# Four layers of graph network and experts on one core: the borders between stages are re-ordered

## The chip, the cores and the metric

The kernel runs on one core of a Trainium2 chip. The metric is the device time of one execution in microseconds (us). A core has five engines, each with its own queue that is worked off in order: TensorE (PE; its weight loads are shown apart as PEld), VectorE (DVE), ScalarE (ACT), GpSimd (POOL) and SyncE (SP, which here only issues transfers). [...]

## The reference, cut to what matters

625 nodes with 512 features each go through four layers. Each layer is a graph network on the normalised nodes, and then a feed-forward part of eight experts:

```
x = x + L0_gnn(layernorm(x)); x = x + L0_ffn(layernorm(x))   # mean of neighbours, batch norm; attention, 8 small experts
x = x + L1_gnn(layernorm(x)); x = x + L1_ffn(layernorm(x))   # 2 attention layers, 4 batch norms, layer norm; top-2 of 8 experts
x = x + L2_gnn(layernorm(x)); x = x + L2_ffn(layernorm(x))   # weighted bases, layer norm, relu; 8 small experts, weights from top 2
x = x + L3_gnn(layernorm(x)); x = x + L3_ffn(layernorm(x))   # graph convolution, batch norm, gelu; top-2 of 8 large experts
# batch norm: over the nodes;  layer norm: over the 512 features of a node
# small experts: out = sum over e of comb[:, e] * (gelu(x @ W1[e] + b1[e]) @ W2[e] + b2[e])
```

All arithmetic that counts for time is in float32.

## The kernel before, in words

**Two layouts.** Node-major data lies with 125 nodes on the partitions, in five tiles (`NT = 5`, `T = 125`) of 512 features. Feature-major data lies with 128 features on the partitions, in four blocks (`KD = 4`) of 626 columns, which products take in two halves of 313 (`HC`). `to_features` turns node-major data with 20 transposes on TensorE, four to a tile, and copies each tile out of PSUM with `evac`, which takes VectorE and ScalarE in turn. `to_nodes` turns the other way, with three PSUM tiles of two banks for the five tiles.

**Layer norm** (`LayerNorm`): `add(t, src)` takes the statistics of a tile on VectorE (`bn_stats` L282, `bn_aggr` L283); when the last tile of a group has come, `close` runs a chain of small instructions (`rstd`, L249 to L260: a square root on ScalarE, then four on VectorE) and writes the normalised tiles, in turn on VectorE (L301) and ScalarE (L307). `GROUPS` is tiles 0 to 2 and then 3 and 4; without it all five close together.

**Batch norm** (`BatchNorm`): `add(k)` takes the statistics of a feature block (L410 to L412). At the end of a group of blocks `apply` runs the same chain and then L428 to L430 (or L423 to L426 for one block), after which the blocks are scaled, on ScalarE (L437) and for some on VectorE (L435). `THREE` groups the blocks as 0 to 2 and 3, `TWO` as 0, 1 and 2, 3. `mm_groups` runs the following products in the same groups, so that they can begin on the first.

**Small experts** (`small_experts`, layers 0 and 2): `ahead(e)` is the first product of an expert (eight matmuls, L380) with its gelu on ScalarE (L828); `expert_out` makes, for each of the five tiles, one matmul (L543) and one addition to `x` on VectorE (L545). Two experts run ahead. The last expert's five tiles feed one layer norm over all tiles.

**Router logits** (`node_logits`): eight matmuls for each half of the columns (L455), two copies (L459), five transposes back (L462), then small work on VectorE: a softmax, the choice of two, or the dispatch.

**The graph network of layer 2** (from L1350): for each tile, products with the adjacency (L1353), five matmuls with another matrix (`mm_nodes`, L388 and L391), four partial products, one on VectorE and one on GpSimd (L1362) and two on ScalarE in 16 instructions (L1367), three additions on VectorE (L1371 to L1373) and one on GpSimd (L1369), the statistics, and, later, `finish(t)`: L1342, L1344, L1346 and the statistics of the next norm.

**Order of the queues.** The program is traced in the order of the code. A scheduler then sets each engine's order when the kernel is built: by its own cost model it takes, whenever an engine is free, the first traced instruction that it believes ready. On the chip that order is fixed, and each engine waits for the head of its queue. PSUM holds four tiles (`pstile`) of two banks each. Weights come as 1 MB chunks through SP's queue, three buffers in turn (`take`).

Of the kernel before, what the change touches and what calls it, by code (L numbers as in the profile page):

```python
# [152 lines left out]
def kernel(  # L153
# [111 lines left out]
    class LayerNorm:  # L265
# [14 lines left out]
        def add(self, t, src):  # L280
            self.src[t] = src
            nc.vector.bn_stats(self.st[:, t, :], src)  # L282
            nc.vector.bn_aggr(self.mv[:, t, :], self.st[:, t, :])  # L283
            for lo, hi in self.groups:
                if t == hi - 1:
                    self.close(lo, hi)
# [37 lines left out]
    def to_features(src, name, scale=None, bias=None):  # L324
# [3 lines left out]
        if bias is None:  # L328
            for t in range(NT):
                ps = pstile("ps_tr")  # L330
                for k in range(KD):
# [3 lines left out]
                     ps[:, 0, :KD * T].rearrange("p (k t) -> p k t", t=T), scale)  # L335
        else:
# [60 lines left out]
    class BatchNorm:  # L397
# [3 lines left out]
        def __init__(self, h, groups, gamma, beta, func):  # L401
# [4 lines left out]
            self.bi = small.tile([P, KD], F32, tag="bn_bi", name="bn_bi")  # L406

# [9 lines left out]
        def apply(self, group):  # L417
# [4 lines left out]
            if len(group) == 1:  # L422
# [3 lines left out]
                nc.vector.tensor_mul(sc, r, gamma)  # L426
            else:
                nc.vector.tensor_mul(sc, r, gamma)  # L428
                nc.vector.tensor_mul(bi, self.mv[:, g, 0], sc)
                nc.vector.tensor_sub(bi, beta, bi)  # L430
# [14 lines left out]
    def node_logits(src, w, bias, name):  # L445


        half = P // 2
        wp = small.tile([P, KD, half], F32, tag="lg_w", name="lg_w", bufs=1)
        nc.gpsimd.memset(wp, 0.0)  # L450
        nc.gpsimd.tensor_copy(wp[:, :, :E], w.rearrange("p (k e) -> p k e", e=E))
        ps = pstile("ps_lg")
        for i in range(2):
            for k in range(KD):
                nc.tensor.matmul(ps[k % 2 * half:(k % 2 + 1) * half, i, :HC], wp[:, k, :],  # L455
                                 src[:, k, i * HC:(i + 1) * HC], start=(k < 2), stop=(k >= 2))
        lT = small.tile([P, NP], F32, tag="lg_T", name="lg_T", bufs=1)
        for i, copy in enumerate((nc.vector.tensor_copy, nc.scalar.copy)):
            copy(lT[:, i * HC:(i + 1) * HC], ps[:, i, :HC])  # L459
        pt = pstile("ps_lt")  # L460
        for t in range(NT):
            nc.tensor.transpose(pt[:T, t // 4, t % 4 * P:(t % 4 + 1) * P], lT[:, t * T:(t + 1) * T],  # L462
                                ident)
        lg = stile(name)
        for i, n in ((0, 4), (1, 1)):
            nc.vector.tensor_reduce(
                lg[:, 4 * i:4 * i + n, :],
                pt[:T, i, :n * P].rearrange("p (t g e) -> p t e g", t=n, g=2)[:, :, :E, :],
                axis=AX.X, op=OP.add)
        if bias is not None:  # L470
            nc.vector.tensor_tensor(lg, lg, bias[:, None, :].to_broadcast([T, NT, E]), op=OP.add)
        return lg
# [65 lines left out]
    def expert_out(blocks, comb, e, ln=None):  # L538

        for t in range(NT):  # L540
            ps = pstile("ps_eo")
            for f, (h, w) in enumerate(blocks):
                nc.tensor.matmul(ps[:T, 0, :], h[:, t * T:(t + 1) * T], w, start=(f == 0),  # L543
                                 stop=(f == len(blocks) - 1))
            nc.vector.scalar_tensor_tensor(x[:, t, :], ps[:T, 0, :], comb[:, t, e:e + 1],  # L545
                                           x[:, t, :], op0=OP.mult, op1=OP.add)
            if ln is not None:
                ln.add(t, x[:, t, :])

# [5 lines left out]
    def rows_out(xn):  # L555

        for part, hbm in by_node(rows_hbm):
            nc.scalar.dma_start(hbm, xn[part])
        return to_features(xn, "xnT")
# [257 lines left out]
    def small_experts(src, comb, b1, layer, hpool, ln):  # L817

        hs, ws = {}, {}

        def ahead(e):
            g, j = divmod(e, 4)
            if j == 0:
                ws[g] = take(2)
            w1 = ws[g][0]
            ps = mm_features([(w1[:, k, j * P:(j + 1) * P], src[:, k, :]) for k in range(KD)])
            hs[e] = hpool.tile([P, NP], F32, tag="h", name="h")
            nc.scalar.activation(halves(hs[e]), ps, AF.Gelu_apprx_tanh, bias=b1[:, e:e + 1])  # L828

        bias = expert_bias(comb, layer)  # L830
        bias.pop(0)()
        for e in range(2):
            ahead(e)
        for e in range(E):
            if e + 2 < E:
                ahead(e + 2)
            for step in bias[3 * e - 3:3 * e] if e else ():
                step()
            expert_out([(hs.pop(e), ws[e // 4][1][:, e % 4, :])], comb, e,
                       ln if e == E - 1 else None)  # L840
# [259 lines left out]
    for o in range(KD):  # L1100
        ps = mm_features([(wl[:, k, o * P:(o + 1) * P], agg[:, k, :]) for k in range(KD)])
        nc.vector.tensor_add(halves(hT[:, o, :]), halves(hT[:, o, :]), ps)
        bn.add(o)
# [48 lines left out]
    gate = softmax8(node_logits(yT, vec("L0_ffn_gate_W"), row("L0_ffn_gate_b"), "lg"))  # L1152
    with tc.tile_pool(name="l1g", bufs=1) as pool:
# [11 lines left out]
        with tc.tile_pool(name="l0h", bufs=4) as hpool:  # L1165
            small_experts(yT, gate, vec("L0_ffn_b1"), 0, hpool, LayerNorm(xn))
# [42 lines left out]
        xT = to_features(xn, "xT")  # L1209
        for l in range(2):  # L1210
            if l == 1:
                normalise()
            with tc.tile_pool(name=f"l1p{l}", bufs=2) as pt_pool, \
                    tc.tile_pool(name=f"l1s{l}", bufs=4) as s_pool:
                (w,) = take(1)
                qT = ttile("qT")
                for o, ps in enumerate(mm_groups(
                        TWO, KD, lambda o, k: w[:, k, o * P:(o + 1) * P], xT)):
# [242 lines left out]
```

## Time and profile before

| | |
|---|---|
| median of 3 runs | 1681.29 us (1680.88 to 1683.44) |
| the profiled execution: its own time, and its span from first to last instruction | 1681.51 us, 1679.7 us |
| PE, DVE, ACT, POOL busy | 1505.1, 673.9, 375.8, 256.1 us |
| mean granted TensorE clock | 0.947 |

The profiled execution took 0.2 us more than the median and 1.8 us more than its own span. The stages that the change touches lie, in us from the start of the span, at about 116 to 151 (layer 0's batch and layer norm), 279 to 384 (its small experts, the norm, the queries of layer 1), 511 to 551 and 694 to 760 (the ends of layer 1's two attention layers), 1015 to 1160 (layer 2) and 1177 to 1223 (layer 3's graph network and logits). The two long stages of routed experts, about 774 to 985 and from 1239 on, and the attention are not touched.

A line of the timeline has: start, duration, engine, line, operation, output<-inputs, shapes, count; in brackets how long the engine was idle before it and what ended that. A line of the table by stretches has the stretch, its length, and the busy time and number of instructions of PE, PEld, DVE, ACT and POOL, then the granted TensorE clock, the share of the DMA engines and GB/s.

### The profile page before, as it was taken

What the parts mean: (1) busy time and instruction counts of PE and PEld (TensorE: products, weight loads), DVE (VectorE), ACT (ScalarE), POOL (GpSimd) and SP (SyncE); (2) the same over time, 40 slices, a digit from 0 to 9 for tenths busy, and PEclk for the clock granted to TensorE, in tenths of its full rate; (3) what the DMA queues carried; (4) which work ended last, traced back from release to release, by engine and by line L of the source; (5) the groups of instructions that cost most, each with busy time, mean ns of one, the idle gap of its engine ahead of it and who ended that gap; (6) DMA issues with size and microseconds to landing.
All of it is one profiled execution on the core that took longest, in us unless ns stands there. A gap on an engine that the chain in (4) does not pass through costs nothing.

```text
span 1679.7 us, 15622 instructions
## 1 busy us (share of the span) xinstructions
PE 1505.1 (90%) x5622; PEld 851.1 (51%) x5622; DVE 673.9 (40%) x1754; ACT 375.8 (22%) x704; POOL 256.1 (15%) x309
## 2 busy tenths in 40 slices
PE   7997999989898989846999969698769999999996
PEld 5774556555565656633444436454534444444443
DVE  9825562454884258463222225655421111111110
ACT  1122272111661046321111115311310000000000
POOL 2030042110540034202111112101000001000010
PEclk8998999999999989967999989799879999999998
DMA  3010200111001100063989732014348888869871
GB/s 137 9 47 26 75 1 26 50 51 53 23 1 42 59 26 1 5 260 126 333 260 351 261 71 93 25 51 175 131 155 291 315 301 304 290 265 362 296 260 50
DMA packets 40213, 237.53 MB, mean 141 GB/s; under 512 B 4781, under 2 KB 4909, under 8 KB 14369
## 3 DMA queue, kind: packets, MB, share of 16 engines
q1 hardware_dynamic: 30775, 215.20, 34.9%
q0 software_dynamic: 6608, 15.99, 4.2%
q10 hardware_dynamic: 2746, 5.25, 1.0%
q8 instruction: 48, 0.79, 0.2%
q14 instruction: 36, 0.29, 0.1%
HBM read 246.52 MB, written 14.26 MB: 155 GB/s over the span
## 4 chain that ended last, share of the span: by engine, by line
PE 69%; DVE 13%; issue 11%; DMA 4%; ACT 2%; POOL 1%; SPq 0%; POOLq 0%; DVEq 0%; ACTq 0%
PE ps_mf L380 13%; PE ps_y L762 10%; PE ps_h L1416 10%; PE ps_mn L388 7%; PE ps_h L1284 5%; PE ps_s L865 4%; PE ps_eo L543 4%; PE ps_o L929 4%; DMA sumsL<-slots,node 3%; PE ps_mg L369 3%; PE ps_p L908 3%; PE ps_tr L332 2%; DVE s L871 2%; DVE ln_st L282 2%; PE ps_t L753 1%
## 5 line engine op out<-in xcount | busy, mean ns | idle before, releaser
L1416 PE MATMUL ps_h<-ring,xgT 128*128 128x512 f32 x624 | 275.8, 597 | 0.8 <-DVE xgT L226 0.8
L762 PE MATMUL ps_y<-ring,hT 128*128 128x512 f32 x536 | 239.3, 593 | 0.9 <-issue 0.9
L1416 PEld LDWEIGHTS ps_h<-ring,xgT 128*128 128x128 f32 x624 | 119.0, 192 | 148.7 <-issue 146.5
L762 PEld LDWEIGHTS ps_y<-ring,hT 128*128 128x128 f32 x536 | 97.5, 190 | 103.4 <-issue 102.5
L894 POOL TENSOR_SCALAR s<-s,rs 125x625 f32<-125x625 f32 (+4 forms) x120 | 103.3, 877 | 292.1 <-DVE rs L891 268.0
L770 POOL DMA_INDIRECT sumsL<-slots,node x27 | 42.7, 1581 | 466.7 <-DVE slots L768 356.0
L1419 ACT ACTIVATE g<-ps_h 128x512 f32<-128x512 f32 x39 | 23.3, 597 | 388.9 <-PE ps_h L1416 357.7
L1284 PE MATMUL ps_h<-ring,xgT 128*128 128x512 f32 x224 | 102.2, 604 | 1.5 <-DVE xgT L226 0.8
L876 ACT ACTIVATE s<-s,mn 125x626 f32<-125x626 f32 (+4 forms) x120 | 87.3, 743 | 54.1 <-DVE mn L871 53.9
L871 DVE CUSTOM_DVE_ANT_0 s<-ps_s,mask 125x626 f32<-125x626 f32 (+4 forms) x120 | 82.6, 718 | 25.9 <-PE ps_s L865 24.1
L865 PE MATMUL ps_s<-kT,qT 64*125 64x313 f32 (+4 forms) x416 | 87.3, 468 | 2.8 <-DVE mn L871 2.8
L332 PE MATMUL ps_tr<-ident,xn 125*128 125x125 f32 x140 | 30.5, 401 | 66.1 <-DVE ln_nb L304 52.3
L226 DVE COPY hT<-ps_t 128x512 f32<-128x512 f32 x26 | 18.0, 692 | 171.5 <-PE ps_t L753 171.5
L1421 DVE TENSOR_TENSOR h<-ps_h,g 128x512 f32<-128x512 f32 x39 | 26.7, 686 | 148.9 <-ACT g L1419 148.9
L908 PE MATMUL ps_p<-ident,s 125*125 125x125 f32 x432 | 66.5, 296 | 13.0 <-POOL s L894 11.0
L908 PEld LDWEIGHTS ps_p<-ident,s 125*125 125x125 f32 x432 | 54.7, 197 | 39.0 <-POOL s L894 27.1
L1284 PEld LDWEIGHTS ps_h<-ring,xgT 128*128 128x128 f32 x224 | 43.1, 194 | 55.9 <-issue 52.9
L543 PE MATMUL ps_eo<-w,h 128*125 128x512 f32 x160 | 70.8, 593 | 0.6 <-ACT h L828 0.6
L886 DVE SCALAR_TENSOR_TENSOR s<-s,cnt 125x626 f32<-125x626 f32 x80 | 67.3, 863 | 9.9 <-ACT s L876 9.8
L929 PE MATMUL ps_o<-pT,v 125*64 125x375 f32 (+2 forms) x448 | 60.1, 413 | 9.0 <-DVE mn L871 4.2
L1007 PE MATMUL ps_a<-dst,src 125*128 125x313 f16 x400 | 58.2, 310 | 6.7 <-DVE dst L1004 5.1
L768 DVE TENSOR_SCALAR slots<-ps_y,gate 128x512 f32<-128x512 f32 x27 | 20.3, 751 | 106.3 <-PE ps_y L762 106.3
(353 smaller groups left out, 2048.2 us busy)
## 6 DMA issues: line engine op xcount, KB each, us to landing
ring<-in_weights SPq DMA_DIRECT2D x195, 1024.0 KB
w<-in_weights SPq DMA_DIRECT2D x27, 1024.0 KB
rows_hbm<-xn ACTq DMA_DIRECT2D x2, 1120.0 KB
sumsL<-x ACTq DMA_DIRECT2D x2, 1120.0 KB
out<-sumsL SPq DMA_DIRECT2D x1, 1250.0 KB
x<-in_x SPq DMA_DIRECT2D x1, 1120.0 KB
x<-sumsL SPq DMA_DIRECT2D x5, 224.0 KB
rows<-in_rows SPq DMA_DIRECT2D x1, 1052.0 KB
```

The source lines that it names most:

```text
L380: nc.tensor.matmul(ps[:, half, :HC], w, r[:, half * HC:(half + 1) * HC], start=(n == 0), stop=(n == last))
L388: nc.tensor.matmul(ps[:T, 0, :width], src[:, k, t * T:(t + 1) * T], w[:, k, :width], start=(k == 0), stop=(k == KD - 1 and extra is None))
L543: nc.tensor.matmul(ps[:T, 0, :], h[:, t * T:(t + 1) * T], w, start=(f == 0), stop=(f == len(blocks) - 1))
L762: nc.tensor.matmul(ys[b][:, 0, :], hT[:, j, :], ring[n % RING][:, j, :], start=(c == 0 and j == 0), stop=(c == nch - 1 and j == 3))
L865: nc.tensor.matmul(ps[hh][:T, i, :w], qT[rr, b, t * T:(t + 1) * T], kT[rr, b, i * w:(i + 1) * w], start=True, stop=True)
L871: nc.vector.tensor_tensor_reduce(s[:, hh, :nb * w].rearrange("p (a c) -> p a c", a=nb), ps[hh][:T, :nb, :w], mask[:, t, :nb * w].rearrange ...
L876: nc.scalar.activation(s[:, hh, :nb * w], s[:, hh, :nb * w], AF.Exp, bias=mn[:, hh:hh + 1], scale=-1.0, accum_out=sm[:, hh:hh + 1] if caus ...
L894: nc.gpsimd.tensor_scalar(s[:, hh, :w], s[:, hh, :w], rs[:, hh:hh + 1], 1.0, op0=OP.mult, op1=OP.mult)
L908: nc.tensor.transpose(pp[:T, hh, j * T:(j + 1) * T], s[:, hh, j * T:(j + 1) * T], ident[:T, :T])
L929: nc.tensor.matmul(po[rr, 0, o:n * T], v[:, j, h * DH:(h + 1) * DH], pT[:, hh, j, o:n * T], start=(j == 0), stop=(j == nk - 1))
L1284: nc.tensor.matmul(ps[:, 0, :], xgT[:, k, :], w1[:, k, :], start=(k == 0), stop=(k == KD - 1))
L1416: nc.tensor.matmul(ps[:, i, :], xgT[:, k, :], w[i][:, k, :], start=(k == 0), stop=(k == KD - 1))
```

## The change

- **Batch norm**: `behind()` puts the VectorE instructions of the blocks that follow a closed group behind the last instruction of that group's chain in VectorE's queue. It is used in all six batch norms.
- **Small experts**: three experts run ahead, not two. Experts 0 to 4 add as before. The last three go tile by tile: expert 5's product is scaled on ScalarE and added to `x` on GpSimd, two tiles ahead; experts 6 and 7 are added on VectorE, then the tile's statistics. The norm closes in two groups.
- **First nodes' products**: `to_features` calls `between` after tile 2. There the products of the first half of the columns are traced, ahead of the transposes of tiles 3 and 4: the logits' (layers 1, 2, 3), two experts' (layer 2), three of four query blocks' (layer 1, whose weights are taken earlier).
- **Layer 1's last norm**: tiles 3 and 4 get their statistics on ScalarE (`add_scalar`, five instructions a tile), their scaling on ScalarE, and gamma and the sum on GpSimd; tiles 0 to 2 stay on VectorE. It closes in two groups.
- **Layer 2's graph network**: the adjacency product and the partial products of tile t + 1 are traced ahead of the other product of tile t; one addition moves from VectorE to GpSimd; the norm closes in groups of 2, 2 and 1; `finish` is called for 0, 1, then 2 and 3, then 4.

The diff, cut to its core:

```diff
 class LayerNorm:
+        def add_scalar(self, t, src, junk):
+            self.src[t] = src
+            acc = small.tile([T, 3], F32, tag="ln_acc", name="ln_acc")
+            nc.scalar.activation(junk, src, AF.Identity, accum_out=acc[:, 0:1])
+            nc.scalar.activation(acc[:, 1:2], acc[:, 0:1], AF.Copy, scale=-1.0 / D)
+            nc.scalar.activation(junk, src, AF.Square, bias=acc[:, 1:2], accum_out=acc[:, 2:3])
+            nc.scalar.activation(self.mv[:, t, 0:1], acc[:, 0:1], AF.Copy, scale=1.0 / D)
+            nc.scalar.activation(self.mv[:, t, 1:2], acc[:, 2:3], AF.Copy, scale=1.0 / D)
+            self.closed(t)
...
 def to_features(src, name, scale=None, bias=None, between=None):
+                if between is not None and t == GROUPS[0][1] - 1:
+                    between(dst)
...
 class BatchNorm:
+        def behind(self):
+            return nullcontext() if self.chain is None else tc.issue_after(self.chain.ins)
...
+    class Logits:
...
+        def half(self, src, i):
...
             for k in range(KD):
-                nc.tensor.matmul(ps[k % 2 * half:(k % 2 + 1) * half, i, :HC], wp[:, k, :],
+                nc.tensor.matmul(self.ps[k % 2 * h:(k % 2 + 1) * h, i, :HC], self.wp[:, k, :],
                                  src[:, k, i * HC:(i + 1) * HC], start=(k < 2), stop=(k >= 2))
+            copy = nc.scalar.copy if i else nc.vector.tensor_copy
+            copy(self.lT[:, i * HC:(i + 1) * HC], self.ps[:, i, :HC])
...
-    def rows_out(xn):
+    def rows_logits(xn, w, bias):
...
+        lg = Logits(w, bias)
+        lg.half(to_features(xn, "xnT", between=lambda xnT: lg.half(xnT, 0)), 1)
+        return lg.result()
...
+    class SmallExperts:
...
+        def half(self, e, src, i):
...
+            for k in range(KD):
+                nc.tensor.matmul(self.ps[e][:, i, :HC], self.ws[g][0][:, k, j * P:(j + 1) * P],
+                                 src[:, k, i * HC:(i + 1) * HC], start=(k == 0), stop=(k == KD - 1))
+            if i == 1:
+                self.hs[e] = self.hpool.tile([P, NP], F32, tag="h", name="h")
+                nc.scalar.activation(halves(self.hs[e]), self.ps.pop(e)[:, :, :HC],
+                                     AF.Gelu_apprx_tanh, bias=self.b1[:, e:e + 1])
...
+        def run(self, src, comb, ln):
...
+            for e in range(E - 3):
+                self.ahead(e + 3, src)
+                for step in bias[3 * e - 3:3 * e] if e else ():
+                    step()
+                for t in range(NT):
+                    add(e, t)
+            yw = ktile("yw")
+            for n in range(NT + 2):
+                if n < NT:
+                    nc.scalar.activation(yw[:, n, :], self.out(E - 3, n), AF.Copy,
+                                         scale=comb[:, n, E - 3:E - 2])
+                    nc.gpsimd.tensor_add(x[:, n, :], x[:, n, :], yw[:, n, :])
+                if n >= 2:
+                    t = n - 2
+                    add(E - 2, t)
+                    add(E - 1, t)
+                    ln.add(t, x[:, t, :])
...
             for o in range(KD):
                 ps = mm_features([(w[:, k, o * P:(o + 1) * P], oT[:, k, :]) for k in range(KD)])
-                nc.vector.scalar_tensor_tensor(halves(hT[:, o, :]), ps,
-                                               vec("L1_gnn_bo", l)[:, o:o + 1],
-                                               halves(xT[:, o, :]), op0=OP.add, op1=OP.add)
-                bn.add(o)
+                with bn.behind():
+                    nc.vector.scalar_tensor_tensor(halves(hT[:, o, :]), ps,
+                                                   vec("L1_gnn_bo", l)[:, o:o + 1],
+                                                   halves(xT[:, o, :]), op0=OP.add, op1=OP.add)
+                    bn.add(o)
...
+        (wq,) = take(1)
+        xT = to_features(xn, "xT", between=lambda src: [query(o, src, 0) for o in range(KD - 1)])
...
-        ln, after = LayerNorm(), LayerNorm(xn, groups=GROUPS)
+        ln, after = LayerNorm(groups=GROUPS), LayerNorm(xn, groups=GROUPS)
         turned = list(to_nodes(xT, TWO))
+        gamma = row("L1_gnn_ln_g")
+        for t, ps in turned[3:]:
+            ln.add_scalar(t, ps, y[:, t, :])
+        for t, ps in turned[:3]:
+            ln.add(t, ps)
+        for t, ps in turned[3:]:
+            nb = small.tile([T, 1], F32, tag="ln_n", name="ln_n")
+            nc.scalar.activation(nb, ln.mean(t), AF.Copy, scale=ln.r[:, t:t + 1])
+            nc.scalar.activation(nb, nb, AF.Copy, scale=-1.0)
+            nc.scalar.activation(y[:, t, :], ps, AF.Identity, scale=ln.r[:, t:t + 1], bias=nb)
+            nc.gpsimd.tensor_mul(y[:, t, :], y[:, t, :], gamma)
+            nc.gpsimd.tensor_add(x[:, t, :], x[:, t, :], y[:, t, :])
...
-        ln = LayerNorm(groups=GROUPS)
+        ln = LayerNorm(groups=((0, 2), (2, 4), (4, NT)))
...
             for b in range(2):
                 for h in range(H):
                     nc.scalar.activation(part[b][:, h, :], ag[:, b, :], AF.Copy,
                                          scale=wv[:, h, b:b + 1])
-            nc.gpsimd.tensor_add(part[3], part[3], part[1])
+                nc.gpsimd.tensor_add(part[3], part[3], part[b])
+            parts[t] = part
+        weighted(0)
+        for t in range(NT):
+            if t + 1 < NT:
+                weighted(t + 1)
+            pr = mm_nodes(xnT, wres, t, extra=(ones16[:6, :T], cbs))
+            for done in ((), (), (0,), (1,), (2, 3))[t]:
+                finish(done)
...
             nc.vector.tensor_add(ov, part[2], pr.rearrange("p (h f) -> p h f", h=H))
-            nc.vector.tensor_add(ov, ov, part[0])
             nc.vector.tensor_add(ov, ov, part[3])
             ln.add(t, o[:, t, :])
-            for done in ((), (), (0,), (1, 2), (3, 4))[t]:
-                finish(done)
+        finish(NT - 1)
...
+        def half(src, i):
+            lg.half(src, i)
+            for e in range(2):
+                experts.half(e, src, i)
+        xnT = to_features(xn, "xnT", between=lambda src: half(src, 0))
+        half(xnT, 1)
+        lg = lg.result()
+        experts.ahead(2, xnT)
```

## The prediction

> **What bounds the kernel now.** I read the page first, then the table by stretches, then the timeline of each border. The chain of waits on the page gives TensorE 69% and VectorE 13%:
>
> ```profile
> PE 69%; DVE 13%; issue 11%; DMA 4%; ACT 2%; POOL 1%; SPq 0%; POOLq 0%; DVEq 0%; ACTq 0%
> ```
>
> The table by stretches shows where TensorE stands idle.
>
> ```profile
> 344.50:367.00 22.50, 17.17 (x50) 9.35 (x50) 19.01 (x36) 5.04 (x7) 4.28 (x4) 0.85 0.25 94
> 511.00:548.00 37.00, 27.72 (x98) 18.79 (x96) 18.92 (x62) 6.87 (x12) 0.10 (x1) 0.91 0.16 57
> 531.00:534.00 3.00, 2.91 (x6) 1.93 (x7) 1.00 (x6) 1.83 (x4) 0.00 (x0) 0.50 0.48 202
> 732.00:758.00 26.00, 11.60 (x56) 9.23 (x56) 18.85 (x56) 5.77 (x10) 0.00 (x0) 0.60 0.76 306
> 1056.00:1080.00 24.00, 9.37 (x44) 6.30 (x45) 17.61 (x48) 5.20 (x11) 1.78 (x3) 0.64 0.12 44
> 1138.00:1160.00 22.00, 16.68 (x51) 8.83 (x50) 18.92 (x36) 5.00 (x8) 3.86 (x3) 0.92 0.49 191
> 1239.20:1484.00 244.80, 244.80 (x651) 114.34 (x652) 28.76 (x43) 21.69 (x38) 15.89 (x13) 0.99 0.80 280
> ```
>
> The routed experts (last row) leave TensorE no idle time, so time won before them moves them forward whole. At the borders TensorE idles for length minus busy: 5.3, 9.3, 14.4, 14.6 and 5.3 us in the longer rows, and by the same table 9.4 at 694 to 732 and 11.1 at 1194 to 1222: 69.4 in all, the most that the change can work on.
>
> **Batch norm (layer 1).** The timeline after the first attention:
>
> ```profile
> 526.96 0.17 DVE L260 RECIPROCAL rs_r<-rs_v 128x3 f32<-128x3 f32 x1
> 528.19 0.87 DVE L1241 SCALAR_TENSOR_TENSOR hT<-ps_mf,vecs,xT 128x626 f32<-128x626 f32 x1 [1.06 <-PE ps_mf L380]
> 528.98 0.15 DVE L428 TENSOR_TENSOR bn_sc<-rs_r,vecs 128x3 f32<-128x3 f32 x1
> 529.95 0.14 DVE L430 TENSOR_TENSOR bn_bi<-vecs,bn_bi 128x3 f32<-128x3 f32 x1
> 530.13 2.51 ACT L437 ACTIVATE hT<-hT,bn_bi,bn_sc 128x626 f32<-128x626 f32 x3 [3.81 <-DVE bn_bi L430]
> 531.09 6.08 PE L369 MATMUL ps_mg<-hT,w 128*128 128x313 f32 x16 [2.94 <-ACT hT L437]
> ```
>
> Block 3's L1241 sits in the queue before L428 and waits 1.06 us for TensorE; ScalarE and then TensorE wait for what is behind it. In layer 0's uninterrupted chain ScalarE starts 0.80 us after L260 (132.42 to 133.22). So it starts at 527.76, 2.37 earlier, and its first block (2.51 / 3) is there at 528.6, where TensorE's last product has just ended (528.15). Nothing is late behind it: L1241's product is not there before 528.19. After the idle 2.94 us the granted clock was 0.50 (531 to 534) and 16 records took 6.08 us; the row of the queries, 64 in 16.91, makes 4.23. With a gap of 0.5 the clock should hold. Block 3 follows: statistics by 530.0, ScalarE free at 530.3, scaled at 532.6, two products to 533.8 against 537.2: 3.4 us. If the clock is low all the same, 2.4. Twice: 6.8 (4.8 to 7.0).
>
> [...]
>
> In the second norm (`TWO`) the chain of blocks 0 and 1 is mixed with blocks 2 and 3 and ends 7.75 us after the first L1254 (539.40 to 547.15). Kept whole it ends after 5.3: blocks 0 and 1 take 3.6 (two times 0.87, 0.47, 0.47 and aggregates), the chain 1.7 (131.49 to 133.22). The next queries start 2.4 earlier. What gets late is blocks 2 and 3, done 11.4 us after instead of 10.3; eight products of 0.53 in each half cover that in layer 0 of the two. In the last one only ten transposes do, and to_nodes ends 0.6 later. 2.4 (0.8 to 2.6); the 0.6 is in the last norm below.
>
> Layers 0 and 3: no interruption today (L251 to L430 run through at 131.49 and 1194.87, the next block's product comes after). Nothing; cover is not needed.
>
> **Small experts' ends.** TensorE's last 15 products start at 1137.76, the transposes 18.4 later (344.33 and 362.69 in layer 0: the same):
>
> ```profile
> 1137.76 13.04 PE L543 MATMUL ps_eo<-w,h 128*125 128x512 f32 x30
> 1156.12 3.77 PE L332 MATMUL ps_tr<-ident,xn 125*128 125x125 f32 x20 [5.32 <-DVE xn L301]
> ```
>
> Tile by tile, tile 2's last product is the 11th: 11 x 0.86 = 9.5. Addition 0.73, statistics 0.86, chain 1.19 (1154.33 to 1155.52), L301 0.55: transposes from 12.9, 5.4 earlier, just as the products end. VectorE then still owes four additions (0.66), two statistics (0.7), two copies out of PSUM (0.68), a chain: tile 3 at 18.7, where today its transposes begin at 20.6. So the end lies between 1.9 earlier, if nothing stands between, and 5.4. In layer 0 twelve query products (0.53 each, 6.3 us) are traced there: copies of tile 2 done at 15.6, products to 21.9, tiles 3 and 4 with three of the four PSUM tiles held and so one after the other to 24.1, 20 products to 34.7, against 39.8 (384.12). That is 5.1; I take 4.0 (1.9 to 5.1) for late copies. In layer 2 the scheduler may pull a node product (3.43) in: 3.5 (1.9 to 5.4).
>
> The added wait: expert 6's addition waits for GpSimd's, and behind it queue expert 7's, the statistics, and TensorE by its four PSUM tiles. x is there after 0.86 + 0.77 (L236, 500 columns with pointers) + 1.4 (L1400, 1396 ns) = 3.1 with hops, the product of expert 6 at 3.4; then 1.4 a tile against TensorE's 2.6. Hidden by the products; uncovered it is 2.2 a tile. The queries' weights are taken earlier, so SP also queues the next two loads earlier; the chunk's buffer is free after expert 3, 8.5 us before these 15 products, and 1 MB at 434 GB/s (715 to 718) takes 2.4. Nothing. Three experts ahead: the same products in another order, nothing. Layer 0's logits: copies and transposes of L1160 fill TensorE, nothing.
>
> **Layer 1's last norm.** ScalarE needs for a tile 0.59 and 0.19 (copy, read of an accumulator), 0.63 and 0.19 (L1129), three small ones of 0.21 and waits: 2.3; two tiles 4.6 after to_nodes. Chain 1.2, scaling 1.2 a tile, GpSimd four times 1.4, statistics, chain: tile 4 is normalised 29.7 us after the first L1254, now 29.9. No gain there, but tiles 0 to 2 come before it, are turned and their logits' half (1.45 us) is done. A trap: engines reading different banks of one PSUM tile wait for one another, as in
>
> ```profile
> 284.04 0.68 DVE L226 COPY cnt<-ps_ct 125x500 f32<-125x500 f32 x1
> 284.76 0.27 ACT L234 COPY cnt<-ps_ct 125x125 f32<-125x125 f32 x1 [1.78 <-DVE cnt L226]
> ```
>
> so VectorE's tile 2 waits for ScalarE's tile 3 (one PSUM tile): its first group closes at about 25 and not 21, still before tile 4. Logits' reduction at 34.1 instead of 36.3 (759.58): 2.0 (-1.0, GpSimd slowed, to 3.0). The transfers of rows stay ahead of the copies in ScalarE's queue, as now.
>
> **Layer 2.** TensorE is full to 1055.6 and stays so. VectorE then works through to 1072:
>
> ```profile
> 1065.15 2.76 PE L332 MATMUL ps_tr<-ident,xn 125*128 125x125 f32 x12 [9.52 <-DVE ln_nb L304]
> 1070.04 0.65 DVE L226 COPY xnT<-ps_tr 128x500 f32<-128x500 f32 x1
> 1070.69 0.65 DVE L226 COPY xnT<-ps_tr 128x500 f32<-128x500 f32 x1
> 1072.80 1.92 PE L332 MATMUL ps_tr<-ident,xn 125*128 125x125 f32 x8 [4.90 <-DVE ln_nb L304]
> 1074.66 3.50 PE L455 MATMUL ps_lg<-xnT,lg_w 128*64 128x313 f32 x16
> ```
>
> From 1051.8 it loses two additions (1.3), and the rest of finish 0 and 1 and a part of tile 4 (3.8), which now fit before; it gains L1342 and a third chain (1.5): 3.6, of which I count 2.5 for waits on the last product. Products of two experts' halves (4.2) and the logits' (1.7) then lie before the last eight transposes, and fill up to the 4.9 idle plus 1.5 around the logits; if the copies come as late as at 1070.04, only 1.5. Sum 4.0 to 8.9; 6.0. GpSimd takes 4.0 a tile (1.47 + 2 x 1.27) under TensorE's 6.15. Beside it VectorE is slow:
>
> ```profile
> L1372 DVE TENSOR_TENSOR o<-o,part x5: 669/1708/1748, 1031.9 to 1060.6; 125x512 f32<-125x512 f32 x5
> ```
>
> That add goes; L1373 may inherit it (1.0 each, hidden under TensorE except the last).
>
> [...]
>
> Layer 3's logits: 0.3 (0 to 0.6), the 0.59 idle before 1216.16.
>
> **Sum.** 6.8 + 2.4 + 4.0 + 3.5 + 2.0 + 6.0 + 0.3 = 25.0 (12.4 to 32.6). The profiled execution took 1681.5 (0.2 over the median): 1656.5, ends 1649 and 1669.
>
> **Rivals.** *Early products hide nothing*: copies out of PSUM stand late in VectorE's queue, as at 1070.04. Then 9.2 from batch norm, 1.9 at each end, 2.5 in layer 2: 15.5, 1666. 0.16. *GpSimd on VectorE's path* (slower): 19 added GpSimd instructions (ten at the ends, four in the norm, five in layer 2) of 1.39 and ten ScalarE feeds of 0.77 are 34.1 us; waited out in full, 1690.6. It decides from 73% of that (25.0). For it: 1708 against 669 ns; against: the products' slack above. 0.06. *All borders close*: half of 69.4 us, 1646.8. 0.08. *Nothing happens* because the queues already run so: 1681, against it the 1.06 us wait; 0.02. My forecast has 0.68. About 0.2%, 3.4 us, is what a measurement of this kernel can tell from no change. Faster 0.91, same 0.03, slower 0.06. The range of the sum, widened to the third rival: 1647 to 1669.
>
> **What would show it.** L428 directly after L260 and a clock near 1 in L369; first transposes 13 us after the last 15 products start; experts' products before the last eight transposes in layer 2. Wrong if L545 waits for GpSimd, if L1372's slowness moves to L1373 or L1344 behind 1052, or if TensorE idles as long at these borders.

## The result and the profile after

The changed kernel takes 1683.81 us (median) against 1682.59 us before: ratio 1.0007, interval 1.0001 to 1.0014. The forecast was 1656.5 us, range 1647 to 1669. The change costs 1.2 us where 25.0 were to be won, and the range is missed by 15 us.

The profiled execution after took 1683.31 us, its span 1681.2 us. The chain of waits on its page gives TensorE less than before and "issue" more:

```profile
PE 65%; issue 15%; DVE 12%; DMA 4%; ACT 2%; POOL 1%; ACTq 0%; SPq 0%; POOLq 0%; DVEq 0%
```

The table by stretches of the changed kernel, each stretch as long as the one shown before and moved to the same work (end of layer 0, layer 1's batch norms, last norm, layer 2's norm, end of layer 2):

```profile
346.15:368.65 22.50, 16.37 (x44) 8.20 (x43) 17.81 (x39) 7.52 (x11) 11.45 (x9) 0.86 0.13 47
515.84:552.84 37.00, 32.27 (x109) 21.48 (x108) 21.13 (x65) 8.72 (x13) 0.10 (x1) 0.92 0.16 57
728.90:754.90 26.00, 8.31 (x34) 6.00 (x35) 16.80 (x55) 9.86 (x29) 5.44 (x4) 0.50 0.73 288
1054.70:1078.70 24.00, 11.89 (x40) 7.71 (x40) 16.27 (x48) 3.49 (x8) 0.00 (x0) 0.64 0.12 44
1137.00:1159.00 22.00, 16.80 (x49) 8.40 (x48) 18.03 (x38) 7.87 (x12) 11.67 (x10) 0.89 0.36 146
```

In the second row TensorE's idle time falls from 9.3 to 4.7 us: the batch norms work. At the two ends it does not fall (5.3 to 6.1, 5.3 to 5.2), and in the last norm it grows (14.4 to 17.7: 1.8 us of that lie inside the turn to nodes, 1.4 ahead of the logits). In layer 2 it falls from 14.6 to 12.1, with the clock at 0.64 as before.

Cut at fixed pieces of TensorE's work, read from the timelines, the spans divide as follows. "Again" is a second profile of the same program, and "alone" the kernel before with `behind()` alone; both are told of below.

| stretch, from mark to mark | before | after | again | alone | forecast |
|---|---|---|---|---|---|
| start to layer 0's attention | 207.58 | +1.59 | -0.01 | -0.64 | 0 |
| to layer 0's last expert product | 149.80 | +0.23 | +0.24 | +0.01 | 0 |
| layer 0's end: to the end of the queries | 26.59 | +4.26 | +3.27 | -0.04 | -4.0 |
| layer 1's two attentions | 289.28 | -2.28 | +1.26 | +0.25 | 0 |
| its two first batch norms | 20.00 | -7.04 | -7.05 | -7.04 | -6.8 |
| second batch norm and queries, l = 0 | 28.65 | -0.87 | -2.35 | -3.92 | -2.4 |
| second batch norm and turn to nodes, l = 1 | 14.42 | +1.02 | +1.02 | +1.03 | +0.6 |
| last norm, to the first transposes | 14.30 | +0.11 | +0.11 | -0.44 | -2.6 |
| its logits and choice | 12.42 | +1.99 | +2.42 | -0.08 | (in the row above) |
| dispatch, routed experts | 247.60 | -0.25 | -0.33 | -0.34 | 0 |
| layer 2 to its last expert product | 140.16 | +0.29 | -1.02 | +0.20 | -6.0 |
| layer 2's end: to the end of the node products | 26.10 | +1.43 | +2.34 | +0.04 | -3.5 |
| layer 3 to its first transposes | 35.85 | -0.20 | -0.19 | +0.01 | 0 |
| its logits and choice | 13.63 | +1.66 | +1.95 | +0.01 | -0.3 |
| dispatch, routed experts | 453.31 | -0.42 | +0.18 | -0.48 | 0 |

The rows sum to the difference of the spans: +1.5, +1.8 and -11.4. The three rows of batch norms come to -6.9, -8.4 and -9.9, where -8.6 was forecast. In the column after, every other part lost: 4.3 at layer 0's end, 2.1 in the last norm and logits, 0.3 in layer 2 and 1.4 at its end, 1.7 in layer 3's logits.

**Batch norm after.** The timeline at the place shown before:

```profile
531.80 0.18 DVE L260 RECIPROCAL rs_r<-rs_v 128x3 f32<-128x3 f32 x1
532.60 2.51 ACT L459 ACTIVATE hT<-hT,bn_bi,bn_sc 128x626 f32<-128x626 f32 x3 [1.44 <-DVE bn_bi L452]
533.57 5.03 PE L386 MATMUL ps_mg<-hT,w 128*128 128x313 f32 x16 [0.57 <-ACT hT L459]
```

ScalarE starts 0.80 us after L260, as forecast, and TensorE waits 0.57 instead of 2.94 us.

**The end of layer 0 after.** L315, L321, L347 and L1344 were L301, L307, L332 and L1260:

```profile
358.11 0.30 ACT L249 ACTIVATE rs_s<-ln_mv,eps 125x3 f32<-125x3 f32 x1 [2.05 <-DVE ln_mv L283]
358.82 0.74 DVE L875 SCALAR_TENSOR_TENSOR x<-ps_eo,sm_p,x 125x512 f32<-125x512 f32 x1
...
361.75 0.14 DVE L260 RECIPROCAL ln_r<-rs_v 125x3 f32<-125x3 f32 x1
...
362.55 2.85 PE L347 MATMUL ps_tr<-ident,xn 125*128 125x125 f32 x12 [3.36 <-DVE xn L315]
362.57 4.03 POOL L1344 TENSOR_TENSOR x<-x,rows 125x512 f32<-125x512 f32 x3 [6.46 <-DVE ln_nb L318]
...
364.28 1.12 DVE L257 TENSOR_TENSOR rs_v<-rs_v,rs_r 125x2 f32<-125x2 f32 x1
...
365.43 1.18 DVE L258 TENSOR_TENSOR rs_v<-rs_v,rs_s 125x2 f32<-125x2 f32 x1
...
367.38 0.67 DVE L226 COPY xT<-ps_tr 128x500 f32<-128x500 f32 x1
...
368.16 8.72 PE L1279 MATMUL ps_mg<-xT,w 128*128 128x313 f32 x24 [2.77 <-issue]
...
376.72 0.59 PE L347 MATMUL ps_tr<-ident,xn 125*128 125x125 f32 x4
```

Four things are to be seen. The first chain takes 3.78 us from L249 to the end of L260, not 1.19: additions of tiles 3 and 4 (L875) run in between. In the second chain L257 and L258 take 1.12 and 1.18 us where 0.15 is usual, while GpSimd works on L1344. The copy of tile 2 (L226) out of PSUM, the memory that TensorE writes (the names with `ps_`), stands behind that chain, and TensorE waits for it 2.77 us. Then 24 query records take 8.72 us (6.4 at the rate before), and tile 3, normalised since 367.4, is turned only at 376.7.

**Layer 1's logits after**, TensorE's timeline:

```profile
747.63 2.76 PE L347 MATMUL ps_tr<-ident,xn 125*128 125x125 f32 x12 [14.41 <-DVE ln_nb L318]
751.84 2.35 PE L484 MATMUL ps_lg<-xnT,lg_w 128*64 128x313 f32 x8 [1.45 <-ACT xnT L234]
754.12 1.39 PE L347 MATMUL ps_tr<-ident,xn 125*128 125x125 f32 x8
756.23 1.27 PE L484 MATMUL ps_lg<-xnT,lg_w 128*64 128x313 f32 x8 [0.49 <-ACT xnT L234]
```

TensorE waits 1.45 us for the copy of tile 2, spends 2.35 on half the logits at a granted clock of 0.50, and only then turns tiles 3 and 4, which ScalarE and VectorE had finished by 750.0. Before, it waited for copies once at this border (0.59 us, ahead of the last transposes); now it waits three times, 1.45, 0.49 and, ahead of the last three of those transposes, 0.51 us.

**Layer 2's norm after**, TensorE's timeline where the idle times of 9.52 and 4.90 us were:

```profile
1065.22 2.75 PE L347 MATMUL ps_tr<-ident,xn 125*128 125x125 f32 x12 [10.92 <-DVE ln_nb L318]
1069.42 2.35 PE L484 MATMUL ps_lg<-xnT,lg_w 128*64 128x313 f32 x8 [1.44 <-DVE ln_mv L283]
1071.70 6.43 PE L853 MATMUL ps_h<-xnT,w 128*128 128x313 f32 x16
1077.97 0.59 PE L347 MATMUL ps_tr<-ident,xn 125*128 125x125 f32 x4
```

The first wait is 1.40 us longer. The early products then fill the second, and the last transposes stand behind them.

### The profile page after: what moved, and what is told of

It is laid out like the page before. It is cut to its first block, busy times and chain, and to the rows that moved or that the text cites. A ratio compares the mean times of both kernels' runs of the same rounds, so it can differ in the third digit from the quotient of the medians.

```text
span 1681.2 us, 15705 instructions
## 1 busy us (share of the span) xinstructions
PE 1506.5 (90%) x5622; PEld 848.3 (50%) x5622; DVE 670.2 (40%) x1752; ACT 390.3 (23%) x739; POOL 281.4 (17%) x328
## 4 chain that ended last, share of the span: by engine, by line
PE 65%; issue 15%; DVE 12%; DMA 4%; ACT 2%; POOL 1%; ACTq 0%; SPq 0%; POOLq 0%; DVEq 0%
PE ps_y L783 10%; PE ps_h L1531 10%; PE ps_mf L397 8%; PE ps_h L1378 5%; PE ps_mn L405 5%; PE ps_h L853 4%; PE ps_s L921 4%; PE ps_o L985 4%; DMA sumsL<-slots,node 3%; PE ps_eo L867 3%; PE ps_p L964 3%; PE ps_mg L386 2%; DVE s L927 2%; PE ps_a L1063 1%; PE ps_t L774 1%
## 5 line engine op out<-in xcount | busy, mean ns | idle before, releaser
L226 DVE COPY hT<-ps_t 128x512 f32<-128x512 f32 x26 | 18.0, 692 | 171.5 <-PE ps_t L774 171.5
L347 PE MATMUL ps_tr<-ident,xn 125*128 125x125 f32 x140 | 28.9, 375 | 61.4 <-DVE ln_nb L318 48.5
L748 POOL DMA_INDIRECT slots<-rows_hbm,node x31 | 30.9, 996 | 205.4 <-PE ps_x L760 87.8
```

## The experiments

**One part alone.** The kernel before, with this in five of the six batch norms; layer 3's, for which nothing was forecast, stays as it was:

```diff
+            with bn.behind():
                 nc.vector.scalar_tensor_tensor(...)
                 bn.add(o)
```

> The kernel before, with behind() alone added in all six batch norms and nothing else changed. Theory (the batch norm part works, the other parts give it back): between the two traces layer 1's batch norms moved by -3.4, -0.9, -3.6 and -2.3 us and the turn to nodes after the last gave 1.0 to 3.3 back, so 7 to 10 us less than before, about 1673. Rival (what batch norm wins is waited out again at the next border, whatever the other parts do): within 2 us of before, about 1681.

1671.85 us against 1682.26: ratio 0.9938 (0.9921 to 0.9954). Column "alone" above: outside the batch norms each border is within 0.5 us of before. So this part is worth 10 us, nothing waits it out again, and the other parts together, with `behind()` in layer 3, cost 12.

**Products behind all five tiles.**

```diff
-                if between is not None and t == GROUPS[0][1] - 1:
+                if between is not None and t == NT - 1:
```

> The changed kernel, with the first nodes' products traced behind the transposes of all five tiles again (between is called after the last tile). Theory (early products stand in TensorE's queue before transposes that are ready, and wait themselves for a late copy of tile 2): layer 0's queries end 3.6 us earlier (no wait for the copy at 367.4, no second run of transposes at 376.7), layer 1's logits 2.0 and layer 3's 1.7 earlier, layer 2's experts 1.0 later: about -6 us, 1677 to 1678. Rival (the early products do hide idle time, and GpSimd in VectorE's way is what costs): not faster, or slower by 2 to 5 us, 1684 to 1689.

1679.15 against 1682.26: ratio 0.9978 (0.9968 to 0.9988); 4.7 us under the changed kernel's median. Layer 0's end takes 28.44 us (30.85 and 29.86 with early products), layer 1's logits 11.97 (14.41 and 14.84), below the 12.42 of before. But layer 3's logits take 16.08, longer still, and layer 2 up to its last expert product has 139.43 (140.45 and 139.14): there the early products neither win nor lose. So the theory is right for two borders of four, with 1.4 to 2.4 us at layer 0's end where it said 3.6, and layer 3 goes against it; the whole stays 1 us above the 1677 to 1678 expected. TensorE's timeline there shows why:

```profile
1214.04 2.36 PE L484 MATMUL ps_lg<-xnT,lg_w 128*64 128x313 f32 x8
1216.98 0.79 PE L492 MATMUL ps_lt<-ident,lg_T 128*125 128x128 f32 x2 [0.59 <-DVE lg_T L487]
1217.70 2.35 PE L484 MATMUL ps_lg<-xnT,lg_w 128*64 128x313 f32 x8
```

Two transposes that wait for VectorE's copy of the first half stand ahead of the second half's products.

**Both copies behind both halves**, on top of that run:

```diff
-            copy = nc.scalar.copy if i else nc.vector.tensor_copy
-            copy(self.lT[:, i * HC:(i + 1) * HC], self.ps[:, i, :HC])
         def result(self):
+            for i, copy in enumerate((nc.vector.tensor_copy, nc.scalar.copy)):
+                copy(self.lT[:, i * HC:(i + 1) * HC], self.ps[:, i, :HC])
```

> The run with the products behind all five tiles, with one more edit: the two copies of the logits out of PSUM are traced behind the products of both halves, as before the change. Theory (both halves are banks of one PSUM tile, so the second half's products wait for VectorE's copy of the first, and the scheduler puts transposes between them; 7.5 us from the first product to the reduction in layer 3, 5.1 before): layer 3's logits 2.4 us earlier than without this edit, 1676 to 1678. Rival (the clock of 0.50 is what costs there): within 0.5 us, 1679.

1676.82 against 1681.61: ratio 0.9969 (0.9959 to 0.9979). The sixteen records run without a break, and layer 3's logits take 14.62: 1.5 of the 2.4 us expected. The rest is the length of these records:

```profile
1211.57 4.44 PE L484 MATMUL ps_lg<-xnT,lg_w 128*64 128x313 f32 x16
```

The same records in the same order took 3.46 before, at a granted clock of 0.66, and 3.03 in a later run of this edit, where the stretch is 13.21; sixteen took 2.33 at 1.00 (below), and eight 2.35 at 0.50 in the changed kernel. By these numbers 4.44 stands for a clock little above 0.50, an estimate. So both theory and rival have a share.

**The first layer norm chain kept whole at the two ends:**

```diff
+                    with ln.behind():
                         add(E - 2, t)
                         add(E - 1, t)
                         ln.add(t, x[:, t, :])
```

> The changed kernel, with the first layer norm chain kept whole at the small experts' ends: VectorE's additions and statistics of tiles 3 and 4 are put behind the last small instruction of the chain of tiles 0 to 2. Theory (the chain is cut up by the additions that follow, 3.8 us from its first to its last instruction where an uninterrupted one takes 1.2): the first transposes come 2.6 us earlier in layers 0 and 2, of which 1 to 2.6 each is kept: 1679 to 1682. Rival (what ends last at these ends is the second chain and the copy of tile 2 behind it, held up by GpSimd's additions): first transposes earlier, but queries and node products within 0.5 us of where they were, 1683 to 1684.

1680.34 against 1682.26: ratio 0.9984 (0.9975 to 0.9994). The first transposes start 1.33 us after the last product instead of 3.36:

```profile
358.93 1.96 PE L352 MATMUL ps_tr<-ident,xn 125*128 125x125 f32 x12 [1.33 <-DVE x L880]
```

What they wait for is now an addition of an expert (L880), which reads a PSUM tile, and no longer the normalised tile. Layer 0's end takes 27.25 us, 2.6 to 3.6 less than with the chain cut; layer 2's 27.06, 0.5 to 1.4 less. The cut chain was a cost.

**GpSimd's additions held back.** A small GpSimd copy reads the normalised tile 3, and the additions that follow each end are queued behind it:

```diff
+        held = nc.gpsimd.tensor_copy(small.tile([T, 1], F32, ...), xn[:, 3, 0:1])
...
+                with tc.issue_after(held.ins):
                     nc.gpsimd.tensor_add(x[:, t, :], x[:, t, :], row("L1_gnn_ln_b"))
```

> The changed kernel; at the small experts' two ends GpSimd's additions to x that follow (L1344, L1517) are put behind a small GpSimd copy that reads the normalised tile 3, so that they no longer run beside VectorE's second chain. Theory (GpSimd's additions hold up VectorE's small instructions with two inputs: L257 and L258 took 1.12 and 1.18 us there, 0.16 without GpSimd, and in layer 2 L315 1.25 instead of 0.55): those go back to 0.16 and 0.55, the second chain is 2.0 us shorter in layer 0 and 2.6 in layer 2; queries 1 to 2 earlier, node products 1 to 1.5 earlier: 1680 to 1682. Rival (these instructions are long because of ScalarE or the clock, or nothing waits for them): the same durations, or 1683 to 1684.

1678.41 against 1681.61: ratio 0.9979 (0.997 to 0.9989), lower than the 1680 to 1682 expected. The two ends together are 3.7 us shorter than in either profile of the changed kernel; the rest lies spread over the other stretches. The timeline at the end of layer 0:

```profile
363.24 0.15 DVE L257 TENSOR_TENSOR rs_v<-rs_v,rs_r 125x2 f32<-125x2 f32 x1
363.42 0.16 DVE L258 TENSOR_TENSOR rs_v<-rs_v,rs_s 125x2 f32<-125x2 f32 x1
...
364.57 6.15 POOL L1347 TENSOR_TENSOR x<-x,rows 125x512 f32<-125x512 f32 x5
```

L257 and L258 are back at 0.15 and 0.16; in layer 2, where they had taken 1.04 and 1.20 and L315 1.25, all three are back at 0.16, 0.16 and 0.55. Layer 2's end takes 24.87 us: 2.7 to 3.6 under the changed kernel and 1.2 under before. Layer 0's takes 29.79, near its two values with early products (30.85, 29.86), since its copy of tile 2 is no longer late but tiles 3 and 4 still wait behind 24 query records. So L257, L258 and L315 were longer with GpSimd's additions beside them than without; how the additions do it, no run shows. Not every VectorE instruction beside L1344 was longer: in the changed kernel L253 (362.93) took 0.16 us and the copy L226 (363.68) 0.68.

**All four edits together:** the four diffs above in one kernel.

> The changed kernel with four edits together: products behind all five tiles, both logits copies behind both halves, GpSimd's additions held back at the two tails, and the first layer norm chain kept whole there. Theory (what the two ends lost is the sum of the cut chain, the additions beside the second chain and the early queries): from the last expert product to the end of the queries layer 0 takes 26.6 us less 0.5 to 2 (before 26.6, changed 30.9), and layer 2 to the end of the node products 24 to 25 us (before 26.1, changed 27.5); with the gains of the products behind all tiles that makes 1670 to 1673. Rival (VectorE's own work on tiles 3 and 4, which is the same in any order, sets the end): 27 us or more in layer 0 and over 26 in layer 2, 1675 or more.

1674.03 against 1681.53: ratio 0.9945 (0.9929 to 0.9962), between the 1670 to 1673 expected and the rival's 1675. Layer 0's end takes 27.95 us and layer 2's 27.51, as the rival had them. With the first chain kept whole, VectorE comes to tiles 3 and 4 later; in layer 2 the scaling of tile 3 begins 6.3 us after the last product, against 4.5 with the additions held back alone. TensorE waits 3.64 us for that scaling: the second chain ends last, and what helps the first delays it. But the rival's reason, that this work is the same in any order, does not hold, since layer 2's end took 24.87 in another order. At layer 0's end a loss of 0.7 us or more is left (27.25 at best, 26.59 before), which no run without the unread products told of below takes away.

**Layer 1's last norm and layer 2's graph network as before**, in the changed kernel:

```diff
-        for t, ps in turned[3:]:
-            ln.add_scalar(t, ps, y[:, t, :])
-        for t, ps in turned[:3]:
+        for t, ps in turned:
             ln.add(t, ps)
...
-        weighted(0)
         for t in range(NT):
-            if t + 1 < NT:
-                weighted(t + 1)
...
```

> The changed kernel, with two borders as before: layer 1's last norm on VectorE alone, and layer 2's graph network with its old order of products, its addition on VectorE, its old groups and its old finish. Theory: neither was worth anything; from the end of the turn to nodes to the first transposes it was 14.3 us before and 14.4 after, and TensorE's idle time ahead of layer 2's transposes was 9.5 before and 10.9 after, so -1 to -2 us, about 1682. Rival (GpSimd's added work is in VectorE's way at these two borders): -4 us or more at the norm, 1679 or less. If three engines did help, it is later by 2 or more there, 1686.

1682.80 against 1682.26: ratio 1.0005 (0.9995 to 1.0015). The norm takes 13.95 us on VectorE alone, 14.41 on three engines: no gain from the three, 0.5 lost. Layer 2's idle time ahead of the transposes is 9.52 as before, 10.92 changed. (The two expectations that follow count 0.35 us more, from the end of the last wide product.)

**Why that wait grew.** First the addition alone, back on VectorE:

```diff
+                if b:
                     nc.gpsimd.tensor_add(part[3], part[3], part[b])
...
+            nc.vector.tensor_add(ov, ov, part[0])
```

> The changed kernel with one edit in layer 2's graph network: the addition that went to GpSimd is on VectorE again; order, groups and finish stay as changed. Theory (GpSimd's three instructions a tile hold up VectorE's with two inputs: L1458 took 1144 ns where L1362 took 760, L1436 990 where L1342 took 741): these go back towards 700 to 750 ns, and TensorE's idle time ahead of the transposes goes from 11.3 us back to 9.9 or less, although VectorE has five instructions more: 1681 to 1682.5. Rival (the third group and the new finish make the tail longer): it stays at 11.3 or grows by the added 0.7, 1684.

1683.25 against 1681.53: ratio 1.0006 (0.9997 to 1.0016). This theory falls. L1458 and L1436 still take 1044 and 1096 ns, and the idle time grows to 12.37 us. Then the groups alone, with the calls of `finish` that go with them:

```diff
-        ln = LayerNorm(groups=((0, 2), (2, 4), (4, NT)))
+        ln = LayerNorm(groups=GROUPS)
-            for done in ((), (), (0,), (1,), (2, 3))[t]:
-                finish(done)
...
             ln.add(t, o[:, t, :])
+            for done in ((), (), (0,), (1, 2), (3, 4))[t]:
+                finish(done)
```

> The changed kernel with one edit in layer 2's graph network: the norm closes in tiles 0 to 2 and 3, 4 and finish is called as before; the new order of products and GpSimd's addition stay. Theory (with groups of 2, 2 and 1 tile 2 waits for tile 3's statistics, and VectorE finishes tile 3 ahead of the chain that the first transposes wait for): TensorE's idle time ahead of the transposes goes from 11.3 us to 9.9 or less, since VectorE has one addition a tile less than in the kernel before. Rival (VectorE's instructions, stretched beside GpSimd, set it whatever the groups are): 11 or more. The whole is within 2 us of the changed kernel, 1681 to 1684, either way.

1683.63 against 1683.11: ratio 1.0003 (0.9993 to 1.0012). The idle time is 9.33 us: the groups of 2, 2 and 1 with their `finish` made it grow. Tile 2 then waits for tile 3's statistics and is finished together with it; that this is the reason is argued from the order, not measured apart. The way to the last expert product got no shorter (140.75 us, against 140.45 and 139.14), since TensorE now waits 3.19 instead of 1.44 us ahead of the logits. VectorE got no faster by the missing addition: the stretched instruction is now L1458, 1424 ns, where L1362 took 760 before.

**The changed kernel once more**, nothing edited.

> The changed kernel once more, with nothing edited. Theory (after an idle time of 3.3 us it is open whether the granted clock falls to 0.50, and the program does not decide it): the stretch from the second batch norm of layer 1's first part to the end of the queries, 27.8 us in the changed kernel's profile and 24.7, 26.3 or 27.8 in the others with the same order and the same 3.27 us of idle time, can come out as any of the three, and the attention (143.0 us) as 143 to 146. The borders' other segments are the same within 0.3 us. Rival (the program decides it): 27.8 and 143.0 again. One of three values by chance would also give 27.8, so only another value decides.

1683.75 us. The queries after the second batch norm, in three profiles with the same order and the same idle time ahead (the run with the old norm and graph network, this one, and the changed kernel's first):

```profile
547.30 17.13 PE L386 MATMUL ps_mg<-xT,w 128*128 128x313 f32 x64 [3.27 <-ACT xT L459]
```

```profile
547.17 18.70 PE L386 MATMUL ps_mg<-xT,w 128*128 128x313 f32 x64 [3.27 <-ACT xT L459]
```

```profile
547.23 20.18 PE L386 MATMUL ps_mg<-xT,w 128*128 128x313 f32 x64 [3.27 <-ACT xT L459]
```

The first 5 us ran at a granted clock of 1.00, 0.66 and 0.50. The program does not decide it: the same one gave 18.70 and 20.18. So one profile is uncertain by up to 3 us in such a stretch. The table's attention rows (-2.28, +1.26) are of this kind: in the first attention, from 424 to 440, the granted clock was 0.79 on average before (0.50 for 6.8 us), 0.89 in the changed kernel's first profile (0.50 for 3.4 us) and 0.72 in its second, and that attention took 144.2, 143.0 and 145.5 us.

**TensorE kept busy.** The kernel before with `behind()` alone, and products that nothing reads ahead of the transposes at five borders:

```diff
+    def warm(n):
+        ps = pstile("ps_wm")
+        with tc.issue_after(last["pe"].ins):
+            for _ in range(n):
+                nc.tensor.matmul(ps[:, 0, :], ident[:T, :], row("L1_gnn_ln_g"), ...)
...
```

> The kernel before with behind() alone, and products that nothing reads (rows of 512 columns into a PSUM tile of their own) put into TensorE's idle time ahead of the transposes at five borders: 5, 15, 10, 5 and 5 of them, and 4 between tiles 2 and 3 in layer 2. Theory (after an idle time of some 5 us the granted clock is 0.50, and the transposes and logits that follow take 1.5 times as long): the clock is 1.00 there, 20 transposes take 2.9 instead of 4.4 us, logits 2.6 instead of 3.5; of 8 us in sum half is on the path: 4 us less than with behind() alone, 1667 to 1669. Rival (the copies and VectorE set the end, TensorE's speed there does not): the same, 1671 to 1673; if the added products hold up the transposes, later.

1669.05 against 1681.61: ratio 0.9926 (0.9909 to 0.9942); the interval overlaps that of `behind()` alone, and the medians differ by 2.8 us. The stretches tell more, from one profile of each. Layer 3 from the end of its aggregation to the choice takes 25.61 us instead of 28.27, layer 1's logits 10.82 instead of 12.34, the two ends 25.44 and 25.17 instead of 26.55 and 26.14; layer 2 up to its last expert product stays. That makes 6.3 us at four borders; the second batch norm and queries took 1.65 us more in this profile. The logits of layer 3, 2.33 us at a granted clock of 1.00 instead of 3.47:

```profile
1203.93 2.33 PE L472 MATMUL ps_lg<-xnT,lg_w 128*64 128x313 f32 x16 [0.45 <-ACT xnT L234]
```

**What the runs speak for, together:** the changed kernel with products behind all tiles, late copies, additions held back, the old last norm and graph network, such products at the borders and, new, in the second batch norms:

```diff
                 with bn.behind():
                     nc.vector.scalar_tensor_tensor(halves(xT[:, o, :]), ps, ...)
                     bn.add(o)
...
+            warm(3)
```

> What the runs so far speak for, in one kernel: the changed kernel with products behind all five tiles, both logits copies behind both halves, GpSimd's additions held back at the two tails, the last norm and layer 2's graph network as before, and products that nothing reads in TensorE's idle time ahead of the transposes at the five borders and in the second batch norms' 3.3 us. Theory (the segments add up): with behind() alone 1671.9; two tails -1 and -2, layer 2's experts -1.9, logits -1.5 and -2.9, and the second batch norm of layer 1's first part always at its best, 24.7 us for the stretch that took 24.7, 26.3 or 27.8: 1661 to 1665. Rival (the borders are bound by VectorE and the copies, and the added products only displace): no better than the kernel before with behind() and such products, 1669.

1660.50 against 1681.84: ratio 0.9868 (0.9851 to 0.9886), 21 us under the kernel before, 23 under the changed one's median and just under the 1661 to 1665 expected. The two ends take 24.10 and 24.07 us, the second batch norm and queries 24.73, the best of its values.

## Why the prediction was wrong

**Batch norm: right, in the mechanism too.** 6.8 forecast, 7.04 measured for the two first ones, with the clock at 1.00 after the gap of 0.57 us; only the 16 records took 5.03 us where 4.23 were counted (from 16.91 us for 64; the row has 17.11, which makes 4.28). After the second one the next queries start 2.3 us earlier, with 2.4 forecast. What is left of that, with the 0.6 for the turn to nodes, came to 0.87, 2.35 or 3.92 less 1.02; the spread is that of the 64 query records: 20.18 us where the granted clock was 0.50 over the first 5 us, 18.70 where it was 0.66, and 17.13, which the run with the old norm and graph network also took, at 1.00.

**Small experts' ends: the step "transposes from 12.9, just as the products end" failed.** Counted like that, from 346.15, which is 13.04 before the last product's end, they came at 16.4: the chain began 0.9 us later than counted and took 3.78. It was taken at the 1.19 us of an uninterrupted one, and the prediction itself listed four additions and two statistics that "VectorE then still owes"; the scheduler put them inside it. Next, "copies of tile 2 done at 15.6": it was 21.9 (368.05), behind a second chain in which L257 and L258 took 2.30 us beside GpSimd's additions, and 0.31 without them. The added work, which the prediction had priced, was hidden as it said: VectorE's additions waited for TensorE alone (all 42.0 us of their wait, by the profile). What stood in the way were additions that were there before and now start as soon as the first group is normalised. The early queries, counted as covering the wait, made it longer. For the two ends 7.5 us of gain were forecast and 5.6 to 5.7 lost. Held back, these additions gave 2.7 to 3.6 us in layer 2.

**Last norm and logits: two terms.** The norm's own gain was put at none in the working, and that held (0.1). The 2.0 came from half the logits done early; they cost 2.0 to 2.4, as the half stands ahead of transposes that are ready.

**Layer 2: "of which I count 2.5" and the products that "fill up to the 4.9 idle".** TensorE's wait for VectorE was 1.4 longer, with the new groups, not 2.5 shorter. The 24 early products did fill the wait, but at a clock of 0.50 for the logits and 0.69 for the experts (6.43 us for sixteen records instead of 4.3), and the last transposes waited behind them until 1078.0. The sum was 0.3 worse or 1.0 better, not 6.0 better.

**The rivals.** *Early products hide nothing* named the right mechanism and priced it at zero; it had a price below zero. The slower rival had the right engine and the wrong instructions. It was the one case in which several borders lose at once, and the range of the sum was widened for the fast rival only, so the range was too narrow. Nor was the idle time all that could be won: with unread products layer 3 became 2.66 us shorter at a clock of 1.00.

## What to carry over

In a queue worked off in order, work moved forward is work put ahead of something: list what stands behind it, when that is ready, and what the moved work itself waits for, before counting it as cover (tile 3, normalised at 367.4, was turned at 376.7). When a chain starts earlier, list what else is then set free on the other engines and in its own queue (L257 and L258 went from 0.15 us to 1.12 and 1.18). A layer norm chain needs the same protection as a batch norm's (3.78 us cut up, 1.19 whole), but the chain to protect is the one that ends last.

## What was not expected of the hardware

After 3.27 us without work, the granted clock was 1.00, 0.66 or 0.50 over the next 5 us, in runs of the same order and even of the same program, which is worth 3.05 us in 64 records. In the changed kernel's first profile the spell at 0.50 lasted 6.8 us (546.6 to 553.4); in its second the mean of 0.66 from 547 to 552, with 1.00 from 552 to 557, makes 3.4 us at 0.50, an estimate. What decides between the values no run shows. Keeping TensorE busy with products that nothing reads was worth 6.3 us over four borders (2.66, 1.52, 1.11 and 0.97) in one profile of each program, and 2.8 between the medians.
